# A decoder layer on one core: context quantised in later groups, feed-forward products between the experts' last steps, transposed input in banks of its own

## The chip, the cores and the metric

The kernel runs on one NeuronCore of a Trainium2 chip. The metric is the time of one execution on the device in microseconds (us). The engines are TensorE (PE in the profile, with its weight loads as PEld), VectorE (DVE), ScalarE (ACT), GpSimd (POOL) and SyncE (SP), which here only issues DMAs.

## The reference

The input is `x` (2 batches of 256 tokens, 512 channels) and a context of 2 x 512 x 512. All is float32. Three blocks follow each other, each on a layer norm of `x` and added to it:

```
x = x + mamba(layernorm(x))        # h = rmsnorm(.) * norm_w; projections of gate, hidden, B, C, dt
                                   # causal convolution of 4 taps + silu on hidden, B, C
                                   # dt = softplus(dt + dt_bias); decays exp(-exp(A_log) * dt) along the tokens
                                   # y = (C B^T masked by the decays) @ (hidden * dt) + D * hidden; y * silu(gate)
                                   # rmsnorm in 8 groups of 1024 channels; out projection 8192 -> 512
x = x + fq(layernorm(x)) @ fq(ctx) # fq(v) = (clip(round(v / s + z), 0, 255) - z) * s
x = x + ffn(layernorm(x))          # H = v @ W.T + b; z = v @ A
                                   # weights of 8 experts from H and z of every second token (softmax, top 2, sigmoid)
                                   # out = H + (z * (weights @ LiMEs)) @ Bmat * 0.5
```

The gate and the hidden part have 8192 channels each (128 heads of 64), so the projections are most of the work.

## The kernel before

The 512 tokens stay on chip. The 8192 hidden channels are cut into 64 **tiles** of 128, in 8 groups of 8. A tile is numbered c = 8g + j; g is its group, and j is its turn in the group. A group has its own B and C (`wbc`, `b`, `c`) and its own norm.

The main loop has one round per tile, c from 0 to 65. Round c works on three tiles at once: it starts tile c (`begin`), convolves, gates and masks tile c-1, and finishes tile c-2 (`heads`, `gated`). The order of the instructions on TensorE, VectorE, ScalarE and GpSimd is the order in which the code calls them (a manual schedule). Only SP's queue is ordered by the framework. [...]

Work of round c in the order of TensorE:

- `begin(c)`: tiles 0 to 8 are projected plainly (L296, 16 records of 512 columns, 6.9 us). The later tiles use seven products of halves instead of eight (L300): four in `begin`, three in `complete`. GpSimd forms the sums of weights for them (`sum_weights`, L354 to L357), and VectorE forms the sums of the products (L385 to L387 in `sum_begun`, L400 and L401 in `sum_complete`).
- one block of the out projection of the group before (L633, `m`), also with seven products, in all turns but one;
- `heads(c-2)` (L508, `py`), which needs the masks `mT` of tile c-2 from GpSimd (L498), and these need the scans `lT` of VectorE (L488) and a multiplication on ScalarE (L492);
- in turn 3 the projection of the next group's B and C (`b`, `c`; L296), and their convolutions on VectorE (`conv_bT`, `conv_cT`; L319);
- `by_tokens(c-1)`: four transposes of `hid` into `pht` (L472). They need the tile's convolution (`conv_h`: L312 on ScalarE, three taps L319 on VectorE) and its silu (L330, ScalarE). `pht`, `c`, and the products `pcb` and `pcr` of B and C (copied by L443 and L454 into `inner`) share one PSUM bank, `misc`;
- `complete(c)`.

VectorE in round c: L400, L401, first scan, taps of tile c-1, L385 to L387, second scan, sums of the block `m`, then `py` (L520), `y` (L523) of tile c-2, and `hc` (L476) out of `pht`.

The ring `w` in SBUF has four buffers of 512 KB. It holds the weights of a tile or of `wbc`. The ring `wo` has three of 1 MB. It holds first the three `soft` tiles of the start, then the weights of the out projection. SP loads `w` and `wo`, and per tile two rows of decays (`dec`, 384 KB each) into a ring of five.

**Context.** The context of 2 x 512 x 512 is quantised in four quarters of 512 KB: loaded as `kvin` (L265), scaled and clipped from below on ScalarE (L268), clipped from above, rounded and shifted on VectorE (L272, L273), and stored to `kvq` in device memory (L274). Before, this happens within the first group, in the ring `wo`. ScalarE's part is called at the end of rounds 2, 5, 6 and 7, VectorE's at the end of the round after each. The quarters are read back at the end of the loop.

**Start.** While `x` is loaded, 24 matmuls of `ones` (`warmup`, L152) run on TensorE. VectorE normalises `x` into `xh` (L179), TensorE transposes it into `pt`, one two-bank tile for each batch (L186), VectorE evicts channels k = 0, 1 (L192) and ScalarE k = 2, 3 (L196) into `hT`, and `pdt` (L199) is the first projection.

**Tail.** After the last group come the context product (`pq`) and the feed-forward product (`pf`, both L799) in four blocks of 128 tokens. The experts' weights `lo` are a chain of some 30 small operations on VectorE, GpSimd and ScalarE. Then TensorE transposes them (`pwT`, L901), VectorE copies (`wT`, L903), TensorE multiplies with the experts (`pmx`, L905), VectorE multiplies with `z` (`zp`, L906), and TensorE adds the last product to each `pf` (L916). VectorE adds `x` (L920), and SP stores.

## Time and profile before

| | |
|---|---|
| median of 3 runs | 875.57 us (874.71 to 876.08) |
| the profiled execution: time, span | 874.9 us, 873.1 us |
| busy TensorE, VectorE, GpSimd, ScalarE | 858.0, 722.9, 629.8, 360.0 us |
| DMA: moved, mean rate | 116.21 MB, 133 GB/s |
| `kvin` load, `kvq` store: issues, median us to landing | 4, 6.4; 4, 2.6 |
| first group (tiles 0 to 8 are plain) | about 16 to 113 us |
| one tile of a later group | about 11.5 us |

A row of the timeline or of the groups names line, engine, operation and `out<-in` with the shapes; the count of records follows an x. A float32 matmul has two records, a transpose one. In brackets stands how long the engine had been idle before, and what ended it. The chain of waits gives start, length and work. In a list of waits the three numbers are the total, the times and the longest, in us. A busy TensorE doesn't say that its records run at their shortest, and a wait counts only where the engine that waits sets the end.

### The profile page before, as it was taken

The numbers are of one execution on the slowest core, as the hardware profiler recorded it, in microseconds if no ns is written. First come the engines' busy times: TensorE is split into PE (matmuls) and PEld (weight loads), VectorE is DVE, ScalarE is ACT, GpSimd is POOL, SyncE is SP. The second block draws the span as 40 slices with busy tenths as digits, with TensorE's granted clock in tenths as the row PEclk, the third lists the DMA queues.
The fourth block names the chain that finished last, engine by engine and source line by source line (L and its number), as shares of the span: only waits on it lengthen the run. The fifth ranks groups of instructions, "written<-read, shape, count | busy, mean of one in ns | idle before, by whom it ended". The sixth has DMA issues, their size and how long they took to land.

```text
span 873.1 us, 12851 instructions
## 1 busy us (share of the span) xinstructions
PE 858.0 (98%) x4368; PEld 643.9 (74%) x4368; DVE 722.9 (83%) x1133; ACT 360.0 (41%) x779; POOL 629.8 (72%) x614
## 2 busy tenths in 40 slices
PE   9999999999999999999999999999999999999997
PEld 7444476788868887788868887788868888885453
DVE  5668998988799888988799888988789888995753
ACT  2445543444444443444444343534444443443220
POOL 2146788997789778997789878997789878973210
PEclk9999999999999999999999999999999999999998
DMA  6835572335333262435333362335433363323001
GB/s 170 291 122 193 190 267 97 127 107 201 123 113 118 107 217 89 134 104 181 134 127 104 120 199 98 129 119 155 159 113 118 107 210 103 121 85 121 0 1 49
DMA packets 54419, 116.21 MB, mean 133 GB/s; under 512 B 7217, under 2 KB 7473, under 8 KB 54354
## 3 DMA queue, kind: packets, MB, share of 16 engines
q1 hardware_dynamic: 54354, 115.39, 40.0%
q8 instruction: 35, 0.57, 0.3%
q14 instruction: 30, 0.25, 0.1%
HBM read 111.83 MB, written 3.54 MB: 132 GB/s over the span
## 4 chain that ended last, share of the span: by engine, by line
PE 81%; DVE 15%; ACT 1%; issue 1%; POOL 1%; DMA 1%; ACTq 0%; POOLq 0%; DVEq 0%
PE xy L300 31%; PE m L633 18%; PE py L508 8%; PE xy L296 5%; PE pht L472 4%; PE po L691 3%; DVE conv_h L319 3%; PE c L296 3%; DVE lT L488 3%; PE pq L799 2%; PE pf L799 2%; PE warmup L152 1%; PE pcb L441 1%; PE b L296 1%; DVE v L386 1%
## 5 line engine op out<-in xcount | busy, mean ns | idle before, releaser
L498 POOL TENSOR_TENSOR mT<-lT,inner 128x768 f32<-128x768 f32 x128 | 232.8, 1819 | 135.4 <-ACT lT L492 122.3
L488 DVE TENSOR_TENSOR_SCAN lT<-dec,seed 128x512 f32<-128x512 f32 x128 | 154.9, 1211 | 0.0
L319 DVE SCALAR_TENSOR_TENSOR conv_h<-xy,cw,conv_h 128x510 f32<-128x510 f32 (+2 forms) x192 | 143.0, 745 | 13.8 <-ACT gate L416 5.3
L633 PE MATMUL m<-wo,yw 128*128 128x256 f32 x672 | 152.2, 379 | 0.0
L633 PEld LDWEIGHTS m<-wo,yw 128*128 128x128 f32 x672 | 126.7, 190 | 17.1 <-DMA wo<-in_out_w 0.4
L492 ACT ACTIVATE lT<-dec,lT 128x128 f32<-128x128 f32 x256 | 88.7, 395 | 121.7 <-DVE lT L488 96.3
L300 PE MATMUL xy<-hT,w 128*128 128x256 f32 x440 | 113.8, 381 | 0.3
L300 PE MATMUL xy<-hs,w 128*128 128x256 f32 x440 | 112.9, 379 | 0.0
L300 PE MATMUL xy<-hs,ws 128*128 128x256 f32 x440 | 103.9, 379 | 0.0
L508 PE MATMUL py<-mT,hc 128*64 128x256 f32 (+1 forms) x1024 | 97.3, 332 | 0.0
L529 POOL TENSOR_TENSOR sqsum<-sqsum,sq 128x512 f32<-128x512 f32 x56 | 72.3, 1291 | 30.4 <-ACT sq L528 26.8
L508 PEld LDWEIGHTS py<-mT,hc 128*64 128x64 f32 x1024 | 63.4, 136 | 40.1 <-issue 15.7
L300 PEld LDWEIGHTS xy<-hs,ws 128*128 128x128 f32 x440 | 83.6, 190 | 11.4
L300 PEld LDWEIGHTS xy<-hs,w 128*128 128x128 f32 x440 | 83.6, 190 | 11.4
L300 PEld LDWEIGHTS xy<-hT,w 128*128 128x128 f32 x440 | 79.2, 190 | 12.9 <-DVE u L387 1.9
L528 ACT ACTIVATE sq<-y 128x512 f32<-128x512 f32 x56 | 35.3, 631 | 100.2 <-DVE y L523 93.0
L312 ACT ACTIVATE conv_h<-xy,cb,cw 128x512 f32<-128x512 f32 x64 | 49.6, 774 | 62.9 <-DVE xy L401 62.1
L520 DVE SCALAR_TENSOR_TENSOR py<-hid,dsk,py 128x512 f32<-128x512 f32 x64 | 47.8, 747 | 24.4 <-PE py L508 24.4
L296 PE MATMUL xy<-hT,w 128*128 128x512 f32 x144 | 63.3, 592 | 0.0
L300 PE MATMUL xy<-hT,ws 128*128 128x256 f32 x220 | 56.5, 379 | 0.0
L400 DVE TENSOR_TENSOR xy<-xy,u 128x256 f32<-128x256 f32 x55 | 23.7, 430 | 37.1 <-PE xy L300 37.0
L330 ACT ACTIVATE hid<-conv_h 128x512 f32<-128x512 f32 x64 | 40.3, 630 | 27.0 <-DVE conv_h L319 26.8
(199 smaller groups left out, 1347.0 us busy)
## 6 DMA issues: line engine op xcount, KB each, us to landing
dec<-decays SPq DMA_DIRECT2D x128, 384.0 KB, 3.4
w<-in_in_w SPq DMA_DIRECT2D x128, 256.0 KB, 3.1
wo<-in_out_w SPq DMA_DIRECT2D x16, 1024.0 KB, 7.4
wbc<-in_in_w SPq DMA_DIRECT2D x16, 256.0 KB, 3.0
kvin<-in_ctx_kv SPq DMA_DIRECT2D x4, 512.0 KB, 6.4
kvq<-kvin SPq DMA_DIRECT2D x4, 512.0 KB, 2.6
kv<-kvq SPq DMA_DIRECT2D x4, 512.0 KB, 3.7
acc<-in_x SPq DMA_DIRECT2D x4, 256.0 KB, 3.2
```

The source lines that it names most:

```text
L296: nc.tensor.matmul(pp, w[:, k, :], hT[:, k, :], start=(k == 0), stop=(k == KD - 1))
L300: nc.tensor.matmul(out, w[:, k, :], h[:, k, :], start=(k == 0), stop=(k == KD // 2 - 1))
L312: nc.scalar.activation(by_batch(self.a[:]), pv, AF.Identity, bias=cb[:, c : c + 1], scale=cw[:, c, 3:4])
L319: nc.vector.scalar_tensor_tensor(av[:, :, d:], pv[:, :, : S - d], cw[:, c, 3 - d : 4 - d], av[:, :, d:], ALU.mult, ALU.add,)
L330: nc.scalar.activation(self.dst, self.a[:], AF.Silu)
L488: nc.vector.tensor_tensor_scan(lT[:, 0:NT, :].rearrange("p t i -> p (t i)"), dec[:, 0:T], seed[:], 0.0, ALU.mult, ALU.add)
L492: nc.scalar.mul(lT[:, NT + b, :], dec[:, T + b * P : T + (b + 1) * P], lT[:, 2 * b, P - 1 : P])
L498: nc.gpsimd.tensor_tensor(m[:], z.lT[n][:], inner[:], ALU.mult)
L508: nc.tensor.matmul(z.py[n * HD : (n + 1) * HD, b * S + s * P : (b + 1) * S], z.hc[:, 2 * b + s, n, :], z.mT[n][:, part, :], start=(s == 0) ...
L520: nc.vector.scalar_tensor_tensor(py[:], hid[:], dsk[:, c : c + 1], py[:], ALU.mult, ALU.add)
L529: nc.gpsimd.tensor_tensor(sqsum[:], sqsum[:], sq[:], ALU.add)
L633: nc.tensor.matmul(o.po[:, t, :], lhs[k][:, t * P : (t + 1) * P], rhs[k], start=(k == 0), stop=(k == GJ // 2 - 1))
```

## The change

There are three parts.

1. **Context.** Quarter q is taken in three steps, one round each, at an early place of the round, ahead of the convolution: the load is called in round 7 + 8q (turn 7 of group q), ScalarE's part in round 8 + 8q (turn 0), VectorE's part and the store in round 9 + 8q (turn 1). So the quarters fall into groups 1 to 4 of the loop, with tiles 8 to 9, 16 to 17, 24 to 25 and 32 to 33. `kvin` now uses the ring `w`.
2. **Tail.** Of the feed-forward product of the last block, k = 0 stays ahead of the experts' end, k = 1 moves behind `pwT`, and k = 2, 3 behind `pmx`.
3. **Start.** Four warm-up matmuls fewer, into another bank. The transposes go into two one-bank tiles for each batch, one that VectorE evicts and one that ScalarE evicts.

On SP, with the ring `wo` free earlier, the first three `wo` loads are now ordered between the decay rows of tiles 3 to 5. The stores `kvq` stand behind the first or second `wbc` load of turn 1, ahead of the weights two tiles on, whose buffer they empty. TensorE has the same instructions but for the four warm-ups; VectorE and ScalarE have the same instructions in another order.

```diff
-WARMUP = 24
+WARMUP = 20
...
-    warmup = ps_y.tile([P, P], F32, tag="py", name="warmup")
+    warmup = ps_out.tile([P, P], F32, tag="po", name="warmup")
...
-            xy = ps_proj.tile([P, 2, T], F32, tag="xy", name=f"pt_{b}")
-            pts.append(xy[:].rearrange("p n s -> p (n s)").rearrange("p (k s) -> p k s", k=KD))
+            if b == 0:
+                halves = [
+                    ps.tile([P, 2, S], F32, tag=tag, name=f"pt_0_{tag}")[:]
+                    for ps, tag in ((ps_misc, "misc"), (ps_y, "py"))
+                ]
+            else:
+                halves = [
+                    ps_proj.tile([P, 2, T], F32, tag="xy", name=f"pt_1_{h}")[:, 0, :].rearrange("p (k s) -> p k s", k=2)
+                    for h in range(2)
+                ]
+            pts.append(halves)
...
-                        pts[b][:, k, t * P : (t + 1) * P], xh[b][:, t, k * P : (k + 1) * P], ident[:]
+                        halves[k // 2][:, k % 2, t * P : (t + 1) * P], xh[b][:, t, k * P : (k + 1) * P], ident[:]
...
     def quantise(n):
-        w = wpool.tile([P, 2, D], F32, tag="wo", name=f"kvin_{n}", bufs=3)
+        w = wpool.tile([P, 2, D], F32, tag="w", name=f"kvin_{n}")
         nc.sync.dma_start(...)
+        yield
         nc.scalar.activation(w[:], w[:], AF.Relu, bias=sc[:, 3:4], scale=rsc[:, 2:3])
-        return w
-
-    def quantised(n, w):
+        yield
         nc.vector.tensor_scalar(w[:], w[:], 255.0, ROUND, ALU.min, ALU.add)
         nc.vector.tensor_scalar(w[:], w[:], ROUND, sc[:, 3:4], ALU.subtract, ALU.subtract)
         nc.sync.dma_start(out=kvq[n], in_=w[:])
+        yield
...
+        feed_forward(3, range(1, 2))
         wT = last.tile([NE, NA], F32, name="wT")
         nc.vector.tensor_copy(wT[:], pwT[:])
         pmx = ps_y.tile([RANK, NA], F32, tag="py", name="pmx")
         nc.tensor.matmul(pmx[:], lim[:], wT[:], start=True, stop=True)
+        feed_forward(3, range(2, KD))
...
         while ends_of:
             ends_of.pop()()
+        q, part = divmod(c - 7, GJ)
+        if 0 <= q < 2 * NB and part <= 2:
+            if part == 0:
+                part_of_context = quantise(q)
+            next(part_of_context)
         if z1:
             start_conv(z1)
...
-        if c - 1 in contexts:
-            quantised(len(contexts) - 1, contexts[c - 1])
-        if c in (2, 5, 6, 7):
-            contexts[c] = quantise(len(contexts))
...
-    for t in range(2, NT):
-        feed_forward(t)
+    feed_forward(2)
+    feed_forward(3, range(1))
     experts(lo)
```

More of the change, by code (lines that the diff above doesn't have):

```diff
@@ L192 @@
             nc.vector.tensor_tensor(
-                hT[:, 0:2, batch], pts[b][:, 0:2, :], nw[:, 0:2].unsqueeze(2).to_broadcast([P, 2, S]), ALU.mult
+                hT[:, 0:2, batch], pts[b][0], nw[:, 0:2].unsqueeze(2).to_broadcast([P, 2, S]), ALU.mult
             )
             for k in range(2, KD):
-                nc.scalar.mul(hT[:, k, batch], pts[b][:, k, :], nw[:, k : k + 1])
+                nc.scalar.mul(hT[:, k, batch], pts[b][1][:, k - 2, :], nw[:, k : k + 1])
             for k in range(KD):
@@ L951 @@
     load_small()
-    states, convs, contexts = {}, {}, {}
+    states, convs = {}, {}
     for c in range(NTILE + 2):
```

## The prediction

> **What bounds the kernel now.** I read the page's busy shares first, then the chain of work that ended last, then who TensorE waited for, then the timelines of the stretches that the diff touches.

> ```profile
> span 873.1 us, 12851 instructions
> ...
> PE 858.0 (98%) x4368; PEld 643.9 (74%) x4368; DVE 722.9 (83%) x1133; ACT 360.0 (41%) x779; POOL 629.8 (72%) x614
> ...
> PE 81%; DVE 15%; ACT 1%; issue 1%; POOL 1%; DMA 1%; ACTq 0%; POOLq 0%; DVEq 0%
> ```

> TensorE is the bound, so time can only come from stretches where it idles or runs work that nothing needs. The chain's 15% on VectorE says that there is a stretch where it isn't TensorE. The waits of TensorE between 40 and 175 us name it:

> ```profile
> PE pht L472 <- ACT hid L330: 1.9, 3, 0.8
> PE pht L472 <- ACT inner L454: 1.9, 1, 1.9
> PE pht L472 <- DVE conv_cT L319: 0.3, 1, 0.3
> PE c L296 <- DVE hc L476: 0.2, 1, 0.2
> PE pht L472 <- ACT inner L443: 0.2, 1, 0.2
> ```

> That is 4.5 us, and from 165 to 800 us only about 2.3 more. The chain in that stretch shows who is late (start, length, work):

> ```profile
> 94.36 1.69 DVE kvin L272
> ...
> 96.08 1.65 DVE kvin L273
> 97.73 1.13 DVE lT L488
> ...
> 102.91 0.27 ACT inner L454
> ...
> 103.22 0.67 PE pht L472 x4
> ```

> The quantising pair stands in VectorE's queue ahead of the scan, and the transposes of `hid` end up waiting. The start and the tail, from the same chain:

> ```profile
> 2.29 8.21 PE warmup L152 x48
> 10.50 1.75 PE pt L186 x16
> 12.25 3.63 PE pdt L199 x16
> ```
> ```profile
> 853.77 8.78 PE pf L799 x20
> 862.55 0.55 PE pwT L901 x4
> ...
> 863.12 0.42 DVE wT L903
> ...
> 863.59 0.63 PE pmx L905 x2
> ...
> 864.24 0.69 DVE zp L906
> ...
> 865.07 4.30 PE pf L916 x8
> ```

> At the start TensorE is busy with warm-ups until 10.50. At the end it idles twice, between `pwT` and `pmx` and between `pmx` and the last `pf`.

> [...] L272 took 0.69 us at 63.96 with GpSimd idle, but 1.77 at 94.28, where GpSimd ran L529 until 95.49. So a quarter's pair costs 1.4 us alone and 3.4 to 3.7 beside GpSimd's long operations. [...] warm-up records start 0.213 us apart until 7.8 us, 5.6 us after the first, and 0.111 apart from there. [...] ScalarE's evictions (L196) began at 12.14, after VectorE's (L192) ended at 12.10.

> **Start.** Four warm-ups less are 8 records of the fast kind: 8 x 0.111 = 0.89, so they end at 9.61. The four `xh` operations (L179) end at 9.1, 9.6, 10.1 and 10.57 and don't move. Batch 0's transposes (half of 1.75) run from 9.65 to 10.52, batch 1's follow the last `xh` from 10.6 to 11.5. VectorE evicts k 0-1 of batch 0 at 10.6 to 11.3, and ScalarE, with a bank and a wait of its own, k 2-3 from 10.55 to 11.45. So `pdt` starts at about 11.5 instead of 12.25, and its matmuls need 16 x 0.216 = 3.46 instead of 3.63, since the second batch's evictions are done at 12.4. `xy_0` starts **0.85** earlier. Its weights were issued at 7.45 and 8.1 and took 3.0: no bound. TensorE is continuous from there to 68 us but for 0.2, so the gain is kept; the decays' chain starts from `pdt` and moves along. Bounds: 0.5 (a transpose waits on `xh` longer) to 0.9.

> **First group.** Four ScalarE operations of 1.23 and four VectorE pairs (1.4, 3.4, 3.4, 3.6) leave tiles 3 to 8; one pair comes back at tile 9. Per stall of TensorE: at 69.55, 0.79 after a pair of 1.40: gone. At 91.91, 0.16, with the 1.23 of L268 ahead of the convolution (84.82): gone. At 103.22, 1.89: without the pair the copy of `inner` is up to 3.4 earlier and TensorE is free at 101.33: gone. At 112.56, 0.36 after the pair at 105.02: gone. Sum 3.20. At 122.59, 0.78: the pair at 114.80 stood between `hc` of tile 7 and the scan of tile 8, and quarter 0 now stands exactly there. What changes is that VectorE isn't late when it arrives: `py` of tile 6 now ends at 109.2, and py, y, hc (0.66, 0.69, 0.60) end at 111.2 instead of 114.88. From the pair's end to `pht` it is 4.11 (122.59 less 118.48). With 3.4 for the pair, `pht` starts at 118.7 (of the old clock, without the 0.85): **3.85** earlier. With a pair of 2.0 TensorE's own work sets 118.05 (4.5 gained), with 4.4, behind two long GpSimd operations, it is 119.7 (2.9 gained). I take **3.7**. After that tiles 10 to 12 run as before, 0.3 of wait on `conv_cT` included.

> **Groups 2 to 4.** ScalarE's 1.23 in turn 0 falls into its wait for the sums of `xy` (1.2 to 1.6 us per turn, 1.56 at 203.77). VectorE's pair in turn 1 comes after L401 and ahead of the scan; behind it wait the taps, `hid` (ScalarE), the masks (GpSimd) and `pht`. VectorE's slack there, tile 17:

> ```profile
> 222.41 0.76 DVE L520 SCALAR_TENSOR_TENSOR py<-hid,dsk,py 128x512 f32<-128x512 f32 x1 [1.06 <-PE py L508]
> ...
> 225.58 0.43 DVE L400 TENSOR_TENSOR xy<-xy,u 128x256 f32<-128x256 f32 x1 [1.09 <-PE xy L300]
> ```

> GpSimd is then in the sums of weights, operations of 0.72[...]: the pair takes about 2.35 from 215.12 to 217.5, and GpSimd loses some 1.2. Taps end at 221.0, `hid` at 221.75; `pht` was due at 222.30: no wait. With 3.4 it would be ready at 222.75, a wait of 0.45. The 2.15 of idle above, and 2.2 more in turn 2 (0.39, 0.69, 1.09), take the lateness up; GpSimd's `sqsum` comes 1.5 later and is level again at the mask of 230.1. Three quarters: **+0.2**, bounds 0 and +1.5 (0.5 each).

> **Queues.** SP still has four loads of 512 KB and four stores; now they use slots of the ring `w`. Tile 9's weights wait for tile 6's projections instead of tile 5's (free at 89, landed by 94, read by GpSimd at 105 or later). Tile 11's wait for the store of quarter 0: pair's end 114.6 + 0.33 + 2.6, then 0.8 to issue and 3.1 to land, 121.4, read at about 124.5. Tile 19's land likewise at 224.4, read after 226. The store blocks SP until VectorE's pair is done, but what stands behind it is a decay row and weights of the next turns. Three `wo` loads of 1 MB move from 100-122 to about 45-60 us, where the DMA engines were 51% busy; the decay rows and weights near them are read 15 us later. Their old late landing (0.4 at 116.3) goes. I cost all of this at nothing; were a weight tile to land behind its sum, TensorE has 7 us more until it reads the sums.

> **Tail.** Ahead of `pwT` stay 14 of 20 records: 853.77 + 14 x 0.439 = 859.9; VectorE's last product for `lo` ended at 859.30, so TensorE still sets it, by 0.6. Then pwT 0.55, two `pf` records 0.88 over a wait of 0.49, pmx 0.63, four records 1.76 over a wait of 0.85. All is TensorE without a gap: the last products start at 853.77 + 8.78 + 0.55 + 0.63 = 863.73 instead of 865.07. **-1.3**, bounds 1.1 and 1.35.

> **Sum.** -0.85 - 3.7 + 0.2 - 1.3 = -5.65. The profiled execution took 874.9 for a span of 873.1, 0.7 under the median of 875.57 and inside the runs' 874.71 to 876.08; it becomes 869.25, the median **869.9**. The bounds together give -2.5 to -6.8; 0.2% is 1.75 us, about what a measurement can tell from no change.

> **Rivals.**
> *The first group's stalls change owner.* ScalarE or GpSimd, 50% and 79% busy from 90 to 125, make `hid` or the masks late once VectorE is not, or the pair at tile 9 meets two long operations and its lateness runs on to the `conv_cT` wait. For it: `pht` waits on ScalarE by name. Against: ScalarE itself waited for VectorE in front of each. Then 1.2 instead of 3.7: 872.4. Chance 0.18.
> *Slower: VectorE's pair is carried to turn 4.* There the transposes wait for `conv_cT` with no slack (L319 ends 261.9, `py` at 262.0), so each us that VectorE brings along costs one. If all 3.4 arrived three times it would be +10.2 - 5.85 = +4.35: 879.9. It decides from 1.95 us carried per quarter. For it: VectorE is 87% busy from 165 to 262. Against: 4.3 us of its idle time lie before turn 3. Chance 0.06.
> *Start and tail don't give.* The clock is let go later with fewer warm-ups, or `pwT` waits for `lo`: only the first group remains, 872.0. Against: the release at 7.8 lies ahead of the new end of 9.6. Chance 0.10.

> **Numbers.** Forecast 0.66. Faster by over 0.2%: 0.65 + 0.15 + 0.08 = 0.88; within 0.2%: 0.01 + 0.03 + 0.02 = 0.06; slower: 0.06. The range 868.4 to 873.2 holds the forecast with its bounds and most of the first and third rival.

> **What would show it.** Right: `pdt` starts near 11.5; no wait of `pht` on `inner` or `hid` before tile 8; `kvin` pairs at about 215 with 2.0 to 2.8 us and no new wait of TensorE in turns 1 to 4; no idle between `pwT` and the last `pf`. Wrong: waits of `pht` on `conv_cT` or `hid` that recur in groups 2, 3 and 4, a wait of GpSimd's sums on weights, or a first group no shorter by 3 us.

## The result, and the profile after

| | before | after |
|---|---|---|
| median (runs) | 875.83 us (6: 874.71 to 876.91) | 868.74 us (6: 868.05 to 869.89) |
| ratio, 95% interval | | 0.9921 (0.9909 to 0.9934) |
| profiled execution: time, span | 874.9, 873.1 us | 869.89, 867.0 us |

The changed kernel is 7.1 us faster in the median; measured again later (e15 below) the ratio was 0.9928 (0.9915 to 0.9940). The profiled spans differ by 6.1. The forecast was 5.65 less than before, 869.9. A run takes longer than the span of its instructions: by 1.7 to 1.9 us in every run of before whose span is on record, by 1.75 to 2.89 in those of the changed kernel. What lies outside the span is in no trace, so below the spans of the runs are used as well; those of the six runs of the changed kernel are 866.3 to 867.2.

The page of the changed kernel, its span, its busy times and the shares of the chain that ended last:

```profile
span 867.0 us, 12832 instructions
...
PE 855.9 (99%) x4360; PEld 641.8 (74%) x4360; DVE 719.0 (83%) x1133; ACT 360.5 (42%) x779; POOL 631.2 (73%) x614
...
PE 85%; DVE 10%; DMA 1%; issue 1%; POOL 1%; ACT 1%; SPq 0%; ACTq 0%; POOLq 0%; DVEq 0%
```

VectorE's share of the chain fell from 15% to 10% and TensorE's rose from 81% to 85%: the stretch that VectorE paced got shorter, but it isn't gone. In the list of TensorE's waits between 36 and 175 us (total, times, longest) 4.5 us have become 0.4:

```profile
PE c L306 <- DVE hc L486: 0.2, 1, 0.2
PE pht L482 <- ACT inner L453: 0.2, 1, 0.2
```

The start in the chain of waits (start, length, work). It no longer begins with the warm-ups but with VectorE's first `xh`, and before that the loads:

```profile
10.00 0.55 PE pt_misc L196 x3
10.55 0.44 PE pt_py L196 x4
10.99 0.91 PE pt L196 x8
11.90 3.46 PE pdt L209 x16
```

And the tail. The lines follow each other with no gap: `pf` records now stand in both waits.

```profile
848.94 6.21 PE pf L809 x14
855.15 0.53 PE pwT L911 x4
855.68 1.06 PE pf L809 x2
856.74 0.54 PE pmx L916 x2
857.28 1.91 PE pf L809 x4
859.19 4.03 PE pf L928 x8
```

The quarters, by tile (minimum/median/maximum in ns, first and last start). Every half but two takes its median or nearly so, and a pair then takes 2.0 us; the first pair, at 110.7, took 0.68 + 2.18, and while its second half ran, GpSimd worked on a mask (`mT`, 110.78 to 113.04, 2.26 us where a mask takes 1.82 on the mean):

```profile
L281 DVE TENSOR_SCALAR kvin<-kvin x4: 683/882/887, 110.7 to 407.8; 128x1024 f32<-128x1024 f32 x4
L282 DVE TENSOR_SCALAR kvin<-kvin,sc x4: 1098/1099/2182, 111.4 to 408.7; 128x1024 f32<-128x1024 f32 x4
```

To split the gain I compare the start of the same TensorE record in both traces: the first `xy` is 0.53 earlier, `pht` of tile 8 4.89, the first `pf` of the tail 4.83, the first of the last products (`pf`, L928) 5.88. The last eight records themselves took 4.03 instead of 4.30, which is not in the change and is taken up below.

### The profile page after: what moved, and what is told of

It reads as the page before. It is cut to its first block, busy times and chain, and to the rows that moved or that the text cites. A ratio compares the mean times of both kernels' runs of the same rounds, so it can differ in the third digit from the quotient of the medians.

```text
span 867.0 us, 12832 instructions
## 1 busy us (share of the span) xinstructions
PE 855.9 (99%) x4360; PEld 641.8 (74%) x4360; DVE 719.0 (83%) x1133; ACT 360.5 (42%) x779; POOL 631.2 (73%) x614
## 4 chain that ended last, share of the span: by engine, by line
PE 85%; DVE 10%; DMA 1%; issue 1%; POOL 1%; ACT 1%; SPq 0%; ACTq 0%; POOLq 0%; DVEq 0%
PE xy L310 32%; PE m L643 18%; PE py L518 9%; PE xy L306 7%; PE pht L482 4%; PE c L306 3%; PE po L701 3%; DVE conv_h L329 2%; DVE lT L498 2%; PE pf L809 2%; PE pq L809 2%; PE pcb L451 1%; PE b L306 1%; DVE acc L652 1%; DMA wo<-in_out_w 1%
## 5 line engine op out<-in xcount | busy, mean ns | idle before, releaser
L508 POOL TENSOR_TENSOR mT<-lT,inner 128x768 f32<-128x768 f32 x128 | 233.4, 1824 | 128.6 <-ACT lT L502 115.6
```

Of the source, the lines that this page charges most:

```text
L508: nc.gpsimd.tensor_tensor(m[:], z.lT[n][:], inner[:], ALU.mult)
```

## The experiments

### Each part alone (e1, e2, e3), and before without the arithmetic (e4)

Three kernels take over one part of the diff each, as shown above in the change: the hunks of `quantise` and of the loop (e1), of the start (e2), of the tail (e3). The fourth is the kernel before with the arithmetic of the context left out:

```diff
-        nc.scalar.activation(w[:], w[:], AF.Relu, bias=sc[:, 3:4], scale=rsc[:, 2:3])
...
-        nc.vector.tensor_scalar(w[:], w[:], 255.0, ROUND, ALU.min, ALU.add)
-        nc.vector.tensor_scalar(w[:], w[:], ROUND, sc[:, 3:4], ALU.subtract, ALU.subtract)
```

> Only the context part (quarters in groups 1 to 4, ring w). Theory 1, VectorE's pairs ahead of the scan hold up TensorE in the first group: TensorE's waits of pht between 40 and 175 us fall from 4.1 to under 0.5, and the kernel is 4.2 to 4.7 us faster (ratio 0.9948 to 0.9954). Rival, the gain needs the earlier start of the other part or comes from the tail: under 2.5 us faster.

> Only the start (20 warm-ups, one-bank tiles). Theory 1, every us gained ahead of xy of tile 0 is kept, since the first group's lateness moves along with it: xy of tile 0 starts 0.5 to 0.85 earlier, 0.5 to 0.85 faster in all. Rival, VectorE's pairs in the first group swallow it: under 0.2 faster.

> Only the tail (feed-forward products between pwT, pmx and the last product). Theory 1, it fills two waits of 0.5 and 0.85: the last products start 1.05 earlier after pwT's side, and the kernel is 1.05 to 1.35 us faster. Rival, the switches between kinds of matmul eat it: 0.5 or less.

> The kernel before, with ScalarE's and VectorE's work on the context left out (the context is loaded and stored unchanged, so the output uses an unquantised context); loads, stores, rings and SP's order stay. Theory 1, the engines' work made the stalls: they go, 4.4 to 5.2 us faster than before. Rival, the transfers or the late wo buffers made them: TensorE's waits stay near 4 us and the time within 1 us of before.

| | median (runs) | ratio to before, 95% interval |
|---|---|---|
| before | 875.45 us (27: 874.09 to 877.87) | |
| e1 context | 872.43 (6: 869.09 to 873.58) | 0.9948 (0.9929 to 0.9966) |
| e2 start | 875.51 (22: 873.56 to 876.79) | 0.9998 (0.9990 to 1.0006) |
| e3 tail | 872.86 (5: 872.74 to 872.98) | 0.9959 (0.9947 to 0.9972) |
| e4 no arithmetic | 870.80 (6: 868.76 to 872.15) | 0.9933 (0.9917 to 0.9948) |

e4 has the old loads, stores and rings and yet lost the first group's waits on `hid` and `conv_cT`; what is left of `pht` in it is 0.2 us on `inner`. So the stalls of the first group were the engines' work, not the transfers of the context. Both engines' parts are left out together in e4; that it is VectorE's pair and not ScalarE's operation rests on the chain of waits, not on a run. The times of the other three don't fit the profile's split: the tail alone gives 2.6 us instead of 1.1 to 1.3, the context alone 3.0 instead of 4.5, the start alone nothing. In e2's trace, though, `xy` starts 0.96 earlier than in before and the last products still 1.03 earlier: what the start wins isn't swallowed by the first group. And the runs of before, e1 and e4 spread over 3 to 4 us, those of e3 over 0.24.

### What the spread is: TensorE's clock in the tail

The mean granted clock of each run goes with its time. The 51 runs of before in the next comparison: 874.86 us on the mean at 0.997 (21 runs), 875.38 at 0.996 (13), 876.51 at 0.995 (10), 877.46 at 0.994 (7). The e1 profile shows where the clock goes, in windows of 2 us (length, then busy PE, PEld, DVE, ACT and POOL; granted clock, DMA share, GB/s):

```profile
860.00:862.00 2.00, 1.43 (x3) 0.69 (x4) 0.72 (x2) 0.00 (x0) 0.00 (x0) 0.91 0.00 0
862.00:864.00 2.00, 2.00 (x4) 0.71 (x3) 1.06 (x2) 0.00 (x0) 0.00 (x0) 0.50 0.34 130
```

At 861.63 the clock falls to half. The last products had started 4.50 us earlier than before's, at 860.57, but the eight records then took 6.15 us instead of 4.30: e1 wins 4.5 and gives 1.85 back. In every profile the time from the clock's release (in before at 7.83, where the warm-up records pass from 0.213 to 0.111 us apart) to its fall is a whole number of 3.413 us: 252 in before (860.16 us), 251 in the changed kernel (856.75), 250 in e1, 252 in e2 and e3, 251 in e4. A stretch of 3.413 us, counted from the release, is called a window below. None of those ahead of a fall was idle throughout: TensorE's waits there were 0.5 and 0.86 us in e1, 0.5 us in all in before (2.91 of 3.41 busy), none in the changed kernel. Weighting each record by its rows (33 of 128 in the last products, 8 in `pmx`), an estimate from the shapes, the window ahead of the fall had 20% of the array in use in e1 (858.2 to 861.6), and in the changed kernel (858.9 to 862.3), with no gap at all, 31%. Hence a theory: the clock falls after a window in which little of the array was in use. The release comes at 7.83 in before and at 8.29 in e1, so where the windows stand differs from run to run, and the same kernel may lose between nothing and some 3 us (an estimate from the 4.0 us over which the 51 runs of before spread). Two kernels test it on before, one on the changed kernel.

e10 and e11: the last products 128 rows deep, on before and on the changed kernel.

```diff
+        nc.gpsimd.memset(fbm[:], 1.0)
...
+        nc.gpsimd.memset(ends["zp"][:], 0.0)
         nc.gpsimd.memset(ends["zp"][RANK : RANK + 1, :], 1.0)
...
-            nc.tensor.matmul(pf, zp[0 : RANK + 1, t * P : (t + 1) * P], fbm[0 : RANK + 1, :], start=False, stop=True)
+            nc.tensor.matmul(pf, zp[:, t * P : (t + 1) * P], fbm[:], start=False, stop=True)
```

e12: fillers in before.

```diff
+        filler = ps_out.tile([P, T], F32, tag="po", name="filler")
+        nc.tensor.matmul(filler[:, 0:S], ones[:], ends["wf"][:, 0, 0:S], start=True, stop=True)
         wT = last.tile([NE, NA], F32, name="wT")
...
         nc.tensor.matmul(pmx[:], lim[:], wT[:], start=True, stop=True)
+        nc.tensor.matmul(filler[:], ones[:], ends["wf"][:, 0, :], start=True, stop=True)
```

> The kernel before, with the last products (L916) made 128 rows deep instead of 33: the added rows of the operand zp are zero, so the output is the same, and order, waits and durations stay. Theory 'rows': TensorE's clock falls to half at the end of a window of 3.413 us in which its array was little used, and products of 33 rows count as little. Then only the 2.6 us from pwT to the last products remain as a low stretch, shorter than a window; the clock should stay up in every run: median 873.9 to 874.5 (ratio 0.9985), spread of the runs under 1 us instead of 3.8, mean granted clock 0.997 or more in all runs. Rival 'idle': the waits of 0.49 and 0.85 make the clock fall; they are all still there: median 875.4, spread 3 to 4 us, runs with a clock of 0.992 to 0.995 among them.

> The changed kernel with the same deeper last products (zero rows, same output). Its waits are filled already, and still its profile shows a fall at 862.31, in a window that held 33-row products. Theory 'rows': no fall before the last record any more; median 868.0 to 868.3, spread under 0.5 us, 0.999 of the changed kernel. Rival 'idle': with no idle left there is nothing to win, and nothing changes: 868.7, spread 1 to 2 us, clock at half from about 862.

> The kernel before with two products whose results nobody reads, of 128 rows: one of 256 columns after pwT, one of 512 after pmx. They fill TensorE's waits of 0.49 and 0.85 with 0.44 and 0.88 us, but spare no work: by order of instructions alone the time is that of before or 0.1 longer (875.5). Theory 'clock': the stretch of little use is cut to the last products, so the clock falls at the very end or not at all: median 874.0 to 874.5, spread under 1 us. This is the part of the tail's measured gain (0.9959, 2.6 us in the median) that isn't order; the order's own part is then the rest, 1.1 to 1.4. Rival 'order only': 875.5 with the spread of 3.8.

| | median (runs) | ratio to before, 95% interval |
|---|---|---|
| before | 875.34 us (51: 874.15 to 878.18) | |
| e10 before, 128 rows | 874.49 (21: 873.58 to 876.39) | 0.9990 (0.9983 to 0.9997) |
| e12 before, fillers | 874.78 (21: 874.04 to 875.47) | 0.9990 (0.9984 to 0.9997) |
| e11 after, 128 rows | 868.45 (5: 868.15 to 870.15) | 0.9920 (0.9906 to 0.9934) |

Work that computes nothing makes before faster, by 0.9 us in e10 and 0.6 in e12 by the medians; by the order of instructions alone neither kernel could be. Of the 51 runs of before none had a mean clock over 0.997; 13 of 21 did in e10 with 0.999 or more, and 15 of 21 in e12 with 0.998 or more. That the clock costs time in the tail is shown. The expectations were too high: a spread under 1 us came in neither (2.8 and 1.4), and e12's median missed its 874.0 to 874.5. In e10 the 13 runs took 874.1 to 874.2 on the mean, the other 8 about 876, and its profile, one of the 8, shows why:

```profile
866.00:868.00 2.00, 2.00 (x4) 0.92 (x3) 0.91 (x2) 0.00 (x0) 0.00 (x0) 0.50 0.34 131
```

At 865.47 the clock fell after a window of 61% busy TensorE, 45% of the array in use, and came back at 868.88, one window (3.41 us) of full rows later. So a fall came after a window with gaps and hardly a record of few rows, as well as after one with no gap and 33 rows (31%, the changed kernel), and my "rows" was too narrow. In e12 the fall came at 867.89, after 2.9 us of the 33-row products, near the end, where it costs little: the spread shrank to 1.4 us. In e11's profile TensorE keeps the full clock to the last record:

```profile
862.00:864.00 2.00, 0.81 (x2) 0.00 (x0) 1.36 (x2) 0.00 (x0) 0.00 (x0) 1.00 0.85 323
```

but there is hardly anything left to win in the changed kernel: 868.45 against 868.74, ratios of 0.9920 and 0.9921. The expected spread under 0.5 us didn't come either (2.0). The profiled execution was the slowest of e11, though its TensorE ended 0.4 earlier than the changed kernel's: its last stores took up to 4.2 us to land instead of 2.1, so this spread isn't the clock's alone.

### VectorE's pair in turn 4 (e5)

```diff
-        q, part = divmod(c - 7, GJ)
+        q, part = divmod(c - 10, GJ)
```

> The changed kernel with each of the three steps of a quarter three rounds later: load in turn 2, ScalarE in turn 3, VectorE's pair in turn 4 of groups 1 to 4. Theory 'slack': the operation costs nothing in turn 1 because VectorE has some 4 us of idle time up to turn 3, and it costs its full length where there is none; in turn 4 the transposes already wait for conv_cT. Four pairs of 2.0 us or more: +8, so 876 to 878 (ratio to before 1.001 to 1.003), with TensorE waiting for VectorE about 2 us in each of groups 1 to 4. Rival 'TensorE hides it anywhere': within 1 us of the changed kernel, 868.7 to 869.7.

Measured: 874.25 us (14 runs: 870.77 to 877.46), ratio to before 0.9986 (0.9973 to 0.9998); 5.5 more than the changed kernel's 868.74, where 876 to 878 was expected. TensorE's waits from the whole run:

```profile
PE pht L482 <- DVE conv_cT L329: 8.3, 4, 2.6
```

Four waits of 1.9, 1.9, 2.0 and 2.6 us, at exactly the place that the slower rival of the prediction named. The pairs took 2.6 to 3.3 us there, their first halves 1.5 to 2.2; 0.7 of each pair didn't reach TensorE. In turns 2 and 3, ahead of the stall, TensorE's records gain about 0.8 against the changed kernel (why is not shown), so by the shift of the records a quarter costs 0.9 to 1.7 us, and not the 2 expected. The other part is the clock: the stall at 356 left 43% of a window in use, the one at 455 26%, and for one window each the clock fell to half, 1.7 us lost each time (half of 3.413, an estimate). The first of them:

```profile
359.00:361.00 2.00, 2.00 (x6) 1.60 (x6) 1.97 (x4) 0.69 (x2) 0.82 (x1) 0.51 0.00 0
```

The last products start 7.3 later than in the changed kernel. A stall of 2 us may thus cost nearly twice its length, by the same estimate. Over all profiles, weighted as above, the windows that led to a fall had at most 45% of the array in use (e10), and those that didn't at least 45% (before, 100.0 to 103.4, 1.53 of 3.41 us busy).

### What is left (e15, e13, e6, e16)

e15 is the changed kernel again. e13 is it without its start, e6 without the arithmetic of the context (the three lines of e4). e16 has the 128 rows of e11 and the quarters a group later:

```diff
-        q, part = divmod(c - 7, GJ)
+        q, part = divmod(c - 15, GJ)
```

> The changed kernel once more, so that the three that follow can be compared with it on one chip: 868.7, ratio to before 0.992.

> The changed kernel without its start: context and tail as changed, start as before (24 warm-ups, two-bank tiles). Theory 'x decides': ten profiles show xy_0 starting 6.24 to 6.25 us after the first xh wherever the start is changed, and 6.38 to 7.06 after it where it isn't (6.38 where the warm-ups end before x is there). The banks give 0.13, the warm-ups 0 to 0.7 by how late x is: on the mean 15.68 against 15.27, so 0.4: this kernel takes 0.4 more than the changed one, about 869.1. Rival 'as predicted': 0.85 more, 869.6. Rival 'no gain', as the start alone measured (0.9998): 868.7.

> The changed kernel without ScalarE's operation and VectorE's pair of the context: the four loads and stores stay, the arithmetic is left out. Theory 'hidden': from tile 12 to the last feed-forward product the traces show 0.15 us of loss, and quarter 0 meets VectorE where TensorE's own work nearly sets the end; 0.2 to 0.4 less than the changed kernel, 868.3 to 868.5. Rival 'a cost spread thin': up to 1.5 less, 867.2, if the pairs lengthen GpSimd's operations and lateness runs on.

> The changed kernel with the quarters one group later (loads in turn 7 of groups 1 to 4, pairs in turn 1 of groups 2 to 5) and the last products 128 rows deep (zero rows, same output). Quarter 0 then stands away from the first group's end, where it took 2.83 us: up to 0.3 less; the clock holds to the last product: up to 0.3 less. Together 868.1 to 868.5, spread under 1 us. If both were worth nothing: 868.7.

| | median (runs) | ratio to before, 95% interval |
|---|---|---|
| before | 875.00 us (9: 874.89 to 877.61) | |
| e15 after again | 869.37 (5: 868.45 to 869.41) | 0.9928 (0.9915 to 0.9940) |
| e13 without the start | 869.02 (5: 868.52 to 869.28) | 0.9926 (0.9914 to 0.9939) |
| e6 without the arithmetic | 867.79 (5: 867.46 to 868.01) | 0.9912 (0.9898 to 0.9925) |
| e16 a group later, 128 rows | 868.02 (4: 867.63 to 868.69) | 0.9917 (0.9903 to 0.9930) |

**The start** doesn't show in the times here either (e13). But four of the five times of e15 stand 2.4 to 2.7 us above their spans, those of e13 1.7 to 1.9. By the spans e13 takes 0.4 more, as theory 'x decides' has it (medians 867.2 and 866.8, with runs that overlap). In the profiles the start shows too, but small. Start of the first `xh` and of the first `xy`, in us:

| start as before | xh | xy | | start changed | xh | xy |
|---|---|---|---|---|---|---|
| before | 8.65 | 15.71 | | after | 8.95 | 15.19 |
| e3 | 8.85 | 15.56 | | e2 | 8.51 | 14.76 |
| e4 | 9.40 | 15.78 | | e11 | 9.35 | 15.60 |
| e10 | 9.04 | 15.42 | | e15 | 9.50 | 15.74 |
| e13 | 9.64 | 16.03 | | e16 | 9.70 | 15.94 |

With the changed start, `xy` follows `xh` by 6.24 or 6.25 each time: it waits for `x`, whose arrival differs by 1.2 us between runs. With the old one it is 6.38 at the least, and up to 7.06 where the warm-ups end after `x` is there. That depends on two things that differ by run: when `x` comes, and when the clock is released, 5.3 to 8.4 us after the start of the span. In e1 and e10 `xh` starts at nearly the same time (8.99, 9.04), but with the release at 8.29 and at 5.31 the warm-ups end at 10.7 and at 9.3, and `xy` follows `xh` by 6.95 and by 6.38. So one-bank tiles give 0.13, and fewer warm-ups 0 to 0.7; over the seven profiles with the old start (e1 and e12 included) the mean is 0.44. The times (e2: between -0.9 and +0.5 us) can't resolve that.

**Quarter 0.** e6 against the changed kernel, from the first `xy` to the last products: TensorE gains 1.27 us, where 0.2 to 0.4 was expected. 0.60 of it comes by 128 us and 0.37 more by 165. e16, which has the arithmetic, but not there, gains the same 0.60 and 0.38. So it is the place of quarter 0 that costs 1.0 us, and the other three cost next to nothing. The chains show it. First the changed kernel:

```profile
113.52 1.21 DVE lT L498
...
118.44 1.13 DVE lT L498
119.57 0.66 DVE py L530
```

then e16, same stretch:

```profile
113.43 3.45 PE m L643 x16
116.88 1.45 PE py L518 x16
...
118.92 6.04 PE xy L310 x28
```

In the changed kernel mostly VectorE still leads the chain between 109 and 122 us. The list of waits doesn't tell it, since TensorE waits by a tenth or two at several places: between 113 and 165 us it is busy for 51.22 us, in e16 for 51.62. In e16 TensorE leads from before 100 to 133.9. That quarter 0 met a long operation of GpSimd there (`mT`, 2.26 us), and its pair was 0.9 longer than the others (2.86 against 2.0), is in the trace; how much of the 1.0 this is was not tried. e16 is the fastest complete version: 868.02 against 869.37 for the changed kernel on the same chip, 1.35 less. The intervals of their ratios to before overlap, and so do the times, between 868.45 and 868.69; the spans of the runs don't (865.1 to 865.8, and 866.0 to 867.0). e16 has two edits; of its gain the traces put 1.0 on the place of quarter 0.

## Why the prediction was right, and where it was not

- **Start, -0.85: too large.** It was 0.53 in this pair of profiles and 0.44 on the mean, and the times don't resolve it. The failed step is "The four `xh` operations ... end at 9.1 ... and don't move": one trace was taken for a constant, and `x` was early in it (`xh` at 8.65, against 8.51 to 9.70). The step "`pdt` starts at about 11.5" came out at 11.90 mainly for that reason. The warm-ups did not end at 9.61 either, but at 8.5, since the clock was released at 5.56 and not at 7.83; TensorE then waited 1.0 us for `xh`. ScalarE's first eviction began at 11.03 while VectorE's ran (10.78 to 11.46); the one-bank tiles' own share is 0.13.
- **First group, -3.7 (2.9 to 4.5): right in kind, a little too small.** `pht` of tile 8 moved by 4.36 beyond the start. The pair took 2.86 instead of the assumed 3.4: its first half was as short as beside an idle GpSimd (0.68), and only the second was long (2.18). The bound of 4.5, "TensorE's own work sets 118.05", held for this record: without the arithmetic `pht` is 4.56 earlier (e4). What the sum left out stands behind it: in the records after `pht` TensorE gains another 0.4 without the pair there, and as much again by 143 us (e6, e16).
- **Groups 2 to 4, +0.2: right.** Pairs of 2.0 us instead of 2.35, which was my estimate. In each of the three quarters two of GpSimd's sums took 1.05 and 1.17 us beside the pair, where 0.73 is usual: GpSimd lost 0.76, not 1.2. No wait of TensorE came that wasn't there before; e6 leaves 0.3 for all three quarters, no more than two traces of the changed kernel differ there (0.34, e15).
- **Queues, nothing: right.** e6 makes the same transfers in the same places and gains by 165 us what e16 gains with quarter 0 elsewhere; so what quarter 0 costs there is the engines' work. SP waited for VectorE's pairs, 12.2 us ahead of the four stores (4.1 at most): it issued the first at 113.62, 0.03 after the pair's end, and the decay row behind it at 115.48. And e4 and e6, both without the arithmetic, one with the old transfers and one with the new, run alike: counted from the first `xy`, TensorE's records differ by 0.07 us at most up to 700 us.
- **Tail, -1.3: right in kind, and the term for order a little too large.** From the first `pf` to the last products it is 10.25 instead of 11.30, so 1.05. The steps took 1.06 and 1.91 where 0.88 and 1.76 were assumed, 0.18 and 0.15 more, at the change from one product to another; e3 shows the same two lengths.
- **What no step had** is the clock. In before it costs between nothing and some 3 us at the end of a run (the estimate above), 0.6 to 0.9 as the difference of medians (e12, e10). In the changed kernel, with the waits filled, hardly any of it is left: e11 takes 0.3 less by the medians. So the terms that were measured, 0.53 + 4.36 - 0.06 + 1.05 = 5.88, and 0.6 to 0.9 for the clock make 6.5 to 6.8, between the 6.3 of e15's ratio and the 7.1 of the first medians. That the forecast of 5.65 is near 5.88 is in part luck: start and tail were 0.6 too large together, the first group and the later ones 0.8 too small. (Its bounds add up to -3.0 at the small end, not to -2.5; nothing hangs on that.)
- **The rivals.** "The first group's stalls change owner" is partly true: not by 2.5 us, but by 1.0, and the owner is still VectorE. "Slower" didn't happen in turn 1, and e5 shows its mechanism at work in turn 4. "Start and tail don't give": about half of what was forecast for the start did not come, the tail came.

## What to carry to other kernels

Work on an engine that isn't the bound costs by where it stands: the same pair of operations cost next to nothing in turn 1 of later groups, 1.0 us at the end of the first group, and 0.9 to 1.7 us in turn 4, the clock not counted; read the chain of waits around the place, not the list of waits alone. Before a cost is read from one trace, ask which of its start times come from a load, since those differ by run (`xh` by 1.2 us here). And a spread of some us between runs of the same kernel is a thing to explain: here, after waits of 0.5 and 0.86 us and products of 33 rows near the end of e1, TensorE's clock fell to half, and eight records took 6.15 us instead of 4.30.
